# A new order for the front of a graph-convolution and expert kernel, and other PSUM banks for three aggregations

## The chip, the cores and the metric

The kernel runs on one core of a Trainium2 chip. A core has a matrix engine (TensorE, PE in the profile; its weight loads are PEld), a vector engine (VectorE, DVE), a scalar engine (ScalarE, ACT), a general one (GpSimd, POOL) and a sequencer that issues transfers (SyncE, SP). Each runs its own instructions in order; they meet through semaphores. Matrix results land in PSUM, in eight banks of 128 rows by 2 KB; all else lives in SBUF. The metric is the device time of one execution in microseconds (us), and lower is better.

## The reference

625 rows x of 1024 numbers pass through two blocks with a residual each. The first is a relational graph convolution over 20,000 edges (source, destination, one of two types), the second a mixture of experts (8 experts, the best 2 of each row, and 2 shared ones). Cut to what matters here:

```python
x = x + gnn(layernorm(x));  x = x + ffn(layernorm(x))

def gnn(h):                                   # h: 625 x 1024
    n = ln_weight * (h * rsqrt(mean(h**2) + 1e-6))
    out = n @ W_root + bias                   # 1024 x 286
    for r in range(2):
        w = (edge_type == r)
        msg = n[src] @ W_rel[r] * w[:, None]
        sums = segment_sum(msg, dst);  cnt = segment_sum(w, dst)
        out = out + sums / maximum(cnt, 1)[:, None]
    return h + elu(out) @ wo
```

## The kernel before

Rows are worked in five tiles of 125. The kernel never gathers messages. It counts edges instead: a matrix CT holds, for each relation, how many edges lead from each source row to each destination row, and the sum over edges becomes a product of CT with the projected rows P = n @ W_rel[r]. CT comes from one-hot matrices. The edge list is cut into 160 chunks of 125 edges; for each chunk DVE makes a one-hot of the source's place in its tile (`ohs`, an equality at L849 and a product at L850) and one of the destination's key (`ohk`, L852), and PE multiplies them into an accumulator `cnt` (L868, two banks). Chunks go in groups of 4 (the first sixteen) and 8, with eight buffers for the one-hots.

The work before 100 us, the front, has these pieces:

- Loads. SP issues edge types and sources, then x's tile 0, W_root, x's tile 1, tiles 2 and 3, tile 4 in two parts, the two W_rel, wo (L545 to L654). ACT issues destinations and ln_weight. POOL issues small ones, among them conv_bias broadcast to 125 rows (L610).
- `edge_columns` (L664): DVE makes rows of keys and sources, PE transposes them into one bank (`p_edge`), ACT and DVE write the three columns `cols` that the one-hots compare with.
- `warm(n)` (L970): n products of a constant with itself into `scrap`, whose result nobody reads. They stand at the start of PE's queue.
- `stats(t)` (L753): DVE takes mean and variance of tile t and `neg`, the negative mean; ACT writes h = x - mean (L765).
- `to_columns(t)` (L789): PE transposes h in eight blocks into two banks, ACT evicts the first four with the ln weight as scale (L801), DVE the other four (L798). The result is `nT`. The row factor 1/std is put in later, because it can be taken out of a product: `scales(a, b)` works it out for a few tiles at once.
- `project(i)` (L886): eight steps of nT with a weight matrix, first W_root for tiles 0 to 4 (i = 0 to 4), then relation 0, then relation 1. Root results become `agg` on DVE with the bias `cb` (L901), the others P in three bf16 parts.
- `aggregate(d, r)` (L904): 15 products of CT and P, divided by the count and added to `agg` (L915). Then `elu`, `elu_columns` and `output_proj`.

Which piece goes where is written by hand. `count_windows` runs over the chunks, and after chunk c it runs what `at(c, ...)` has put there: stats and to_columns of tile t, project i, and so on (L987 to L1021). The build then orders the instructions of each engine by its own estimate, within the dependencies and within `tc.issue_after`, which holds an instruction behind another; so an instruction's place may differ from the program's by some steps. `stats(0)` stands behind the edge columns, the first one-hots behind `stats(0)`, `stats(1)` behind tile 0's eviction.

PSUM has a ring of three banks `acc` (scrap, projections, later the output), one of three `mm` (transposes, aggregations) and two for `cnt`. Before `aggregate(4, 1)` the pool is closed and a new one opened with five `acc` and three `mm` (L1031 to L1033), over the same eight banks.

## Time and profile before

| | us |
|---|---|
| median of 3 runs | 304.25 (303.66 to 304.46) |
| the profiled execution, whole | 303.7 |
| its span, first to last instruction | 301.4 |
| PE busy | 290.8 |
| DVE busy | 168.4 |
| ACT busy | 107.5 |
| first transposes of x (tile 0) start | 10.62 |
| project(0) starts | 11.79 |
| aggregate(4, 1) starts | 100.16 |

An execution is some 2.3 us longer than its span. Busy time counts an engine's instructions, weight loads apart; matrix products overlap, so that a busy PE may still hide short waits between its products. In lists by time the columns are start, duration, engine, line, operation, output and inputs, shape, number, and in brackets the idle time before and what ended it. Line numbers are those of the kernel before.

### The profile page before, as it was taken

The numbers are of one execution on the slowest core, as the hardware profiler recorded it, in microseconds if no ns is written. First come the engines' busy times: TensorE is split into PE (matmuls) and PEld (weight loads), VectorE is DVE, ScalarE is ACT, GpSimd is POOL, SyncE is SP. The second block draws the span as 40 slices with busy tenths as digits, with TensorE's granted clock in tenths as the row PEclk, the third lists the DMA queues.
The fourth block names the chain that finished last, engine by engine and source line by source line (L and its number), as shares of the span: only waits on it lengthen the run. The fifth ranks groups of instructions, "written<-read, shape, count | busy, mean of one in ns | idle before, by whom it ended". The sixth has DMA issues, their size and how long they took to land.

```text
span 301.4 us, 4682 instructions
## 1 busy us (share of the span) xinstructions
PE 290.8 (96%) x1649; PEld 194.9 (65%) x1649; DVE 168.4 (56%) x465; ACT 107.5 (36%) x246; POOL 45.2 (15%) x98
## 2 busy tenths in 40 slices
PE   8799999999999799999999999999999999999993
PEld 6687777787889534376777887887843334444452
DVE  5999999998327668756883122212223211255921
ACT  2455118355334432155123244638359311000000
POOL 9500000000000014240131212210003222200000
PEclk9999999999999999999999999999999999999998
DMA  7999910000009999965999253340057555479442
GB/s 243 304 318 393 421 65 2 0 2 1 0 17 340 348 348 391 400 195 182 348 396 410 86 203 96 114 141 3 0 190 276 221 209 210 191 291 385 161 138 73
DMA packets 27408, 61.15 MB, mean 203 GB/s; under 512 B 2176, under 2 KB 16007, under 8 KB 27375
## 3 DMA queue, kind: packets, MB, share of 16 engines
q1 hardware_dynamic: 21806, 43.77, 40.7%
q0 software_dynamic: 5280, 16.69, 15.7%
q10 hardware_dynamic: 294, 0.35, 0.5%
q8 instruction: 15, 0.25, 0.3%
q14 instruction: 13, 0.10, 0.1%
HBM read 42.76 MB, written 18.81 MB: 204 GB/s over the span
## 4 chain that ended last, share of the span: by engine, by line
PE 93%; DVE 4%; ACT 1%; issue 0%; ACTq 0%
PE p_pr L891 20%; PE p_h L1359 13%; PE p_yj L1417 13%; PE p_o L1472 11%; PE p_sh L1137 10%; PE p_y L952 6%; PE p_agg L909 6%; PE p_x L1340 3%; PE p_t L795 3%; PE cnt L868 2%; PE p_y L956 2%; PE p_hT L1371 1%; PE scrap L972 1%; PE p_gate L1085 1%; PE p_o L1474 1%; DVE ln_4s L727 0%
## 5 line engine op out<-in xcount | busy, mean ns | idle before, releaser
L891 PE MATMUL p_pr<-wg,nT 128*125 128x286 f32 x240 | 62.5, 409 | 0.0
L891 PEld LDWEIGHTS p_pr<-wg,nT 128*125 128x125 f32 x240 | 43.2, 187 | 11.3 <-ACT nT L801 0.2
L1359 PE MATMUL p_h<-w1a,xsT 128*128 (+2 forms) x176 | 40.0, 380 | 0.0
L1417 PE MATMUL p_yj<-w2a,hjT 128*128 (+2 forms) x88 | 38.6, 594 | 0.0
L1472 PE MATMUL p_o<-sw,shT 128*125 128x512 f32 (+1 forms) x88 | 36.1, 553 | 0.0
L1137 PE MATMUL p_sh<-h2T,sw 128*128 128x313 f32 (+1 forms) x128 | 35.2, 428 | 0.0
L1359 PEld LDWEIGHTS p_h<-w1a,xsT 128*128 128x128 f32 (+2 forms) x176 | 28.7, 168 | 7.4 <-issue 0.5
L1137 PEld LDWEIGHTS p_sh<-h2T,sw 128*128 128x128 f32 x128 | 23.6, 189 | 8.6 <-issue 0.2
L1417 PEld LDWEIGHTS p_yj<-w2a,hjT 128*128 128x128 f32 (+2 forms) x88 | 14.4, 168 | 22.4 <-issue 22.4
L1472 PEld LDWEIGHTS p_o<-sw,shT 128*125 128x125 f32 x88 | 16.4, 187 | 16.9 <-issue 16.2
L1421 DVE COPY ys<-p_yj 128x512 f32<-128x512 f32 x15 | 10.4, 692 | 28.7 <-PE p_yj L1417 26.5
L1363 DVE COPY hj<-p_h 128x256 f32<-128x256 f32 x11 | 4.7, 425 | 30.8 <-PE p_h L1359 30.8
L909 PE MATMUL p_agg<-P,CT 125*125 125x287 bf16 x150 | 20.1, 287 | 1.6 <-DVE agg L915 1.6
L966 POOL DMA_DIRECT2D x1d<-xh x10 | 5.3, 532 | 98.5 <-DVE xh L959 98.5
L909 PEld LDWEIGHTS <-CT 125*125 125x125 bf16 x150 | 18.5, 136 | 2.5 <-issue 2.0
L1425 POOL DMA_INDIRECT yt<-ys,row x11 | 10.8, 984 | 50.5 <-DVE ys L1421 50.5
L952 PE MATMUL p_y<-wo_t,eT 128*125 128x512 f32 x40 | 18.1, 595 | 0.0
L1332 POOL DMA_INDIRECT xs<-h2d,tok x11 | 11.2, 1015 | 45.0 <-PE p_x L1340 30.9
L1374 ACT ACTIVATE hjT<-p_hT,vT 128x128 f32<-128x128 f32 (+2 forms) x34 | 8.7, 332 | 24.5 <-PE p_hT L1371 24.5
L1344 DVE COPY xsT<-p_x 128x512 f32<-128x512 f32 x11 | 7.6, 692 | 17.4 <-PE p_x L1340 13.8
L1448 DVE SCALAR_TENSOR_TENSOR x<-p_o,x 125x512 f32<-125x512 f32 (+1 forms) x11 | 6.9, 641 | 16.3 <-PE p_o L1474 16.3
L1359 PE MATMUL p_h<-w1m,xsT 128*64 128x256 f32 (+1 forms) x96 | 14.7, 381 | 0.0
(302 smaller groups left out, 424.0 us busy)
## 6 DMA issues: line engine op xcount, KB each, us to landing
w1a<-in_L_ffn_W_dram SPq DMA_DIRECT2D x8, 1024.0 KB, 10.5
w2a<-in_L_ffn_W_dram SPq DMA_DIRECT2D x8, 1024.0 KB, 4.8
yt<-zero SPq DMA_DIRECT2D x2, 2560.0 KB
g<-yt SPq DMA_DIRECT2D x10, 512.0 KB, 6.7
sw<-in_L_ffn_sW_dram SPq DMA_DIRECT2D x4, 1024.0 KB, 5.0
x<-x1d SPq DMA_DIRECT2D x5, 500.0 KB
wg<-in_L_gnn_W_rel_dram SPq DMA_DIRECT2D x2, 1144.0 KB, 19.1
x1d<-xh POOLq DMA_DIRECT2D x5, 448.0 KB, 6.7
```

The source lines that it names most:

```text
L795: nc.tensor.transpose(pv[:, k, :], row[:, at : at + 128], ident[:TP, :TP])
L891: nc.tensor.matmul(p[:TP, :F], nT[:, k, m * TP : (m + 1) * TP], wg[:, k, r, :], start=(k == 0), stop=(k == KD - 1))
L909: nc.tensor.matmul(p[:TP, : F + 1], CT[:, m, at : at + TP], P[:, m, r, i], start=(m == 0 and i == 0), stop=(m == NT - 1 and i == 2))
L952: nc.tensor.matmul(ps[s][:TP, :], eT[:, k, :], wo_t[:, k, s * 512 : (s + 1) * 512], start=(k == 0), stop=False)
L1137: nc.tensor.matmul(p[:, : z - a], sw1[:, i, k, t * 128 : (t + 1) * 128], h2T[:, k, a:z], start=(k == 0), stop=(k == KD - 1))
L1332: nc.gpsimd.indirect_dma_start(out=xs, out_offset=None, in_=h2d, in_offset=bass.IndirectOffsetOnAxis(ap=tok[:, j : j + 1], axis=0))
L1340: nc.tensor.transpose(p[:, k * 128 : (k + 1) * 128], xs[:, at : at + 128], ident)
L1359: nc.tensor.matmul(p[a:b, :H], xsT[j][:, k, a:b], w1m[j, a][:, 0, k, :] if a else w1a[:, bass.ds(e, 1), k, :], start=(k == 0), stop=(k == ...
L1417: made = nc.tensor.matmul(p[a:b], hjT[:, j, k, a:b], w2m[j, a, k][:, at] if a else w2a[:, bass.ds(e, 1), k, at], start=(k == 0), stop=(k = ...
L1421: nc.vector.tensor_copy(y[:, at], p)
L1425: sent.append(nc.gpsimd.indirect_dma_start(out=yt, out_offset=bass.IndirectOffsetOnAxis(ap=row[:, j : j + 1], axis=0), in_=y, in_offset=No ...
L1472: nc.tensor.matmul(p[:TP, :n], shT[:, i, k, own], sw2[:, i, k, at], start=(i == 0 and k == 0), stop=False)
```

## The change

Six edits, made together:

- Loads: x's tile 1 is loaded ahead of W_root, and W_root comes in two halves.
- The bias is loaded once as a single row (`cb1`, by ACT's queue) and spread over 125 rows by a product with a row of ones, evicted by ACT; the broadcast load on POOL is gone.
- Edge lists: sources and keys are transposed into two banks. The columns of the sources are now worked out in a function of their own, `source_columns`, which is issued behind `stats(0)`, and all on DVE.
- The first two tiles: `stats(0)` is held behind the last cast of the edge rows alone. For tiles 0 and 1 h is written in two pieces, 384 columns by ACT and 640 by DVE.
- Order: `to_columns(0)` follows 22 warming products instead of 40 and a first group of one-hots; the one-hots of group 0, `stats(1)`, `scales(0, 2)` and `project(0)` stand ahead of the first count product. Later pieces move to other chunks.
- Banks: `aggregate(1, 1)`, `(3, 1)` and `(4, 1)` take a bank of the ring `acc` instead of `mm`.

```diff
+    cb1 = fbig.tile([1, F], F32, name="cb1")
+    nc.scalar.dma_start(cb1, conv_bias.rearrange("(o f) -> o f", o=1))
...
-    def load_w(r, w):
-        nc.sync.dma_start(wg[:, :, r, :], w.rearrange("(k p) f -> p k f", p=128))
+    def load_w(r, w, *ks):
+        for k in ks or (slice(0, KD),):
+            nc.sync.dma_start(wg[:, k, r, :], w.rearrange("(k p) f -> p k f", p=128)[:, k])

     load_x(0, 1)
-    load_w(R, W_root)
     load_x(1, 1)
+    load_w(R, W_root, slice(0, KD // 2), slice(KD // 2, KD))
...
     cb = gbig.tile([TP, F], F32, name="cb")
-    nc.gpsimd.dma_start(cb, bcast_rows(conv_bias, TP))
+    one = fbig.tile([1, TP], F32, name="one")
+    nc.vector.memset(one, 1.0)
...
-        p = ps_mm("p_edge")
+        got = nc.vector.tensor_copy(rowf[:, 0], rows_i["src"])
+        ps = [ps_acc("p_edge"), ps_mm("p_edge_k")]
...
+    def source_columns(v, behind):
+        q = fbig.tile([EP, 2, EC], F32, name="q")
+        with tc.issue_after(behind.ins):
+            nc.vector.tensor_scalar(q[:, 0], v, -float(TP // 2), 1.0 / TP, op0=ALU.add, op1=ALU.mult)
         nc.vector.tensor_scalar(q[:, 1], q[:, 0], ROUND, -ROUND, op0=ALU.add, op1=ALU.add)
-        nc.scalar.copy(column(cols[:, SP_]), pairs(q[:, 2]))
+        nc.vector.scalar_tensor_tensor(cols[:, SP_], pairs(q[:, 1]), -float(TP), pairs(v),
+                                       op0=ALU.mult, op1=ALU.add)
...
+        p = ps_mm("p_cb")
+        nc.tensor.matmul(p[:TP, :F], one, cb1, start=True, stop=True)
+        nc.scalar.copy(cb, p[:TP, :F])
...
-            with tc.issue_after((second[0] if t > 1 else evicted[1] if t else behind).ins):
+            with tc.issue_after((second[0] if t > 1 else first if t else behind).ins):
...
+        own, rest = (slice(0, 384), slice(384, D)) if t < 2 else (slice(0, D), None)
...
-            moved = nc.scalar.activation(h, xh[:TP, t, :], AF.Identity, bias=neg)
+            moved = nc.scalar.activation(h[:, own], xh[:TP, t, own], AF.Identity, bias=neg)
+        if rest:
+            with tc.issue_after(last.ins):
+                last = nc.vector.tensor_scalar(h[:, rest], xh[:TP, t, rest], neg, None, op0=ALU.add)
...
-        p = ps_mm(f"p_agg_{d}_{r}")
+        p = (ps_acc if r and d in (1, 3, 4) else ps_mm)(f"p_agg_{d}_{r}")
...
-    warm(40)
-    ahead = stats(0)
+    warm(22)
+    source_columns(sources, stats(0))
+    to_columns(0, hs[0], nT, True)
...
-    for t, (c0, c1) in enumerate(((0, 3), (4, 9), (13, 19), (16, 22), (20, 26))):
+    for t, (c0, c1) in enumerate(((0, 3), (6, 11), (9, 14), (13, 18))):
         if t:
-            at(c0, stats, t)
-        at(c1, to_columns, t, None, nT, True)
+            at(c0, stats, t + 1)
+        at(c1, to_columns, t + 1, None, nT, True)
...
-    at(6, scales, 0, 2)
-    at(18, scales, 2, 4)
-    at(21, scales, 4, NT)
-    for i, c in enumerate((7, 15, 21, 24, 28, 46, 64, 82, 100, 118, 134, 148)):
-        at(c, project, i)
+    at(10, scales, 2, 4)
+    at(14, scales, 4, NT)
+    for i, c in enumerate((3, 12, 15, 20, 38, 56, 74, 92, 110, 128, 146)):
+        at(c, project, i + 1)
...
+    oh_s, oh_k, first = one_hots(0, GROUPS[0])
+    made[0] = oh_s, oh_k
+    stats(1)
+    scales(0, 2)
+    project(0)
     count_windows(between)
```

The one-hots' code is moved into a function `one_hots`, in which the destination's one-hot is held behind the source's product, and the first two groups behind tile 0's eviction and tile 1's statistics.

More of the change, by code (lines that the diff above doesn't have):

```diff
@@ L671, in edge_columns, with pairs @@
                                        op0=ALU.mult, op1=ALU.add)
-        nc.vector.tensor_copy(rowf[:, 0], rows_i["src"])
-        p = ps_mm("p_edge")
-        pv = p[:EP, : 2 * EC].rearrange("p (a j c) -> p a j c", a=2, j=2)
+        got = nc.vector.tensor_copy(rowf[:, 0], rows_i["src"])
+        ps = [ps_acc("p_edge"), ps_mm("p_edge_k")]
         for a in (0, 1):
             for j in range(2):
-                nc.tensor.transpose(pv[:, a, j, :], rowf[:, a, j * EP : (j + 1) * EP], ident[:EH, :EH])
-        wide = [EP, EH, 2, 2]
-        def column(v):
-            return v.rearrange("p (c j) b -> p c j b", j=2)
-        def pairs(v):
-            return v.rearrange("p j c -> p c j")[:, :, :, None].to_broadcast(wide)
-        with tc.issue_after(table.ins):
-            nc.scalar.copy(column(cols[:, KW_]), pairs(pv[:, 1]))
-        q = fbig.tile([EP, 3, 2, EH], F32, name="q")
-        nc.vector.tensor_scalar(q[:, 0], pv[:, 0], -float(TP // 2), 1.0 / TP, op0=ALU.add, op1=ALU.mult)
+                nc.tensor.transpose(ps[a][:EP, j:EC:2], rowf[:, a, j * EP : (j + 1) * EP], ident[:EH, :EH])
+        with tc.issue_after(table.ins):
+            nc.scalar.copy(cols[:, KW_], pairs(ps[1][:EP, :EC]))
+        return got, ps[0][:EP, :EC]
+    def pairs(v):
+        return v[:, :, None].to_broadcast([EP, EC, 2])
+    def source_columns(v, behind):
+        q = fbig.tile([EP, 2, EC], F32, name="q")
+        with tc.issue_after(behind.ins):
+            nc.vector.tensor_scalar(q[:, 0], v, -float(TP // 2), 1.0 / TP, op0=ALU.add, op1=ALU.mult)
         nc.vector.tensor_scalar(q[:, 1], q[:, 0], ROUND, -ROUND, op0=ALU.add, op1=ALU.add)
-        nc.vector.scalar_tensor_tensor(q[:, 2], q[:, 1], -float(TP), pv[:, 0], op0=ALU.mult, op1=ALU.add)
-        nc.scalar.copy(column(cols[:, SP_]), pairs(q[:, 2]))
-        return nc.vector.tensor_scalar(column(cols[:, VV_].bitcast(I16)), pairs(q[:, 1]), 4096.0, 7168.0,
+        nc.vector.scalar_tensor_tensor(cols[:, SP_], pairs(q[:, 1]), -float(TP), pairs(v),
                                        op0=ALU.mult, op1=ALU.add)
+        nc.vector.tensor_scalar(cols[:, VV_].bitcast(I16), pairs(q[:, 1]), 4096.0, 7168.0,
+                                op0=ALU.mult, op1=ALU.add)
     flagf = const.tile([1, 2], F32, name="flagf")
@@ L826, in sparse_kernel, with one_hots, both, halves @@
     ends = [R * TP * min(DB * (b + 1), NT) for b in range((NT + DB - 1) // DB)]
+    made = {}
+    def one_hots(c0, g):
+        oh_s = oneh.tile([EP, MAXG, 128], F16, tag="oh_s", name=f"ohs_{c0}")
+        oh_k = oneh.tile([EP, MAXG, KR], F16, tag="oh_k", name=f"ohk_{c0}")
+        def both(what, n):
+            return [EP, g, n // 2, 2], cols[:, what, c0 : c0 + g][:, :, None, :].to_broadcast([EP, g, n // 2, 2])
+        def halves(v):
+            return v.rearrange("p g (a b) -> p g a b", b=2)
+        row = iota[:EP].rearrange("p (a b) -> p a b", b=2)
+        shape, key = both(SP_, 128)
+        os = halves(oh_s[:, :g, :])
+        with ExitStack() as order:
+            if c0 < 8:
+                order.enter_context(tc.issue_after((second[0] if c0 else evicted[1]).ins))
+            nc.vector.tensor_tensor(os, row[:, None].to_broadcast(shape), key, op=ALU.is_equal)
+        last = nc.vector.tensor_tensor(os, os, both(VV_, 128)[1], op=ALU.mult)
+        shape, key = both(KW_, KR)
+        with tc.issue_after(last.ins):
+            nc.vector.tensor_tensor(halves(oh_k[:, :g, :]), row[:, None, :SPAN].to_broadcast(shape), key,
+                                    op=ALU.is_equal)
+        return oh_s, oh_k, last
     def count_windows(between):
@@ L831, in count_windows @@
         for g in GROUPS:
-            oh_s = oneh.tile([EP, MAXG, 128], F16, tag="oh_s", name=f"ohs_{c0}")
-            oh_k = oneh.tile([EP, MAXG, KR], F16, tag="oh_k", name=f"ohk_{c0}")
-            def both(what, n):
-                return [EP, g, n // 2, 2], cols[:, what, c0 : c0 + g][:, :, None, :].to_broadcast([EP, g, n // 2, 2])
-            def halves(v):
-                return v.rearrange("p g (a b) -> p g a b", b=2)
-            order = ExitStack()
-            if c0 == 0:
-                order.enter_context(tc.issue_after(ahead.ins))
-            elif c0 == 8:
-                order.enter_context(tc.issue_after(second[0].ins))
-            row = iota[:EP].rearrange("p (a b) -> p a b", b=2)
-            shape, key = both(SP_, 128)
-            os = halves(oh_s[:, :g, :])
-            nc.vector.tensor_tensor(os, row[:, None].to_broadcast(shape), key, op=ALU.is_equal)
-            nc.vector.tensor_tensor(os, os, both(VV_, 128)[1], op=ALU.mult)
-            shape, key = both(KW_, KR)
-            nc.vector.tensor_tensor(halves(oh_k[:, :g, :]), row[:, None, :SPAN].to_broadcast(shape), key,
-                                    op=ALU.is_equal)
-            order.close()
+            oh_s, oh_k = made.pop(c0) if c0 in made else one_hots(c0, g)[:2]
             for i in range(g):
@@ L975, in sparse_kernel @@
     warm(24)
-    behind = edge_columns()
+    behind, sources = edge_columns()
     transpose_lnw()
-    warm(40)
-    ahead = stats(0)
+    warm(22)
+    source_columns(sources, stats(0))
+    to_columns(0, hs[0], nT, True)
     after = {c: [] for c in range(EC)}
```

## Prediction, made blind

> **What bounds the kernel now.** I read four views in turn: busy time by engine, who waited for whom on TensorE (PE), the first 32 us in order of time, and the chain of work that ended last. Busy time first:

> ```profile
> PE 290.8 (96%) x1649; PEld 194.9 (65%) x1649; DVE 168.4 (56%) x465; ACT 107.5 (36%) x246; POOL 45.2 (15%) x98
> ```

> PE is the bound, so a change pays only where PE idles or does useless work. Its waits up to 106 us (us in total, times, longest):

> ```profile
> PE cnt L868 <- DVE ohs L850: 1.7, 1, 1.7
> PE p_agg L909 <- DVE agg L915: 1.6, 1, 1.6
> PE cnt L866 <- DVE nil L824: 1.5, 1, 1.5
> ```

> The 1.5 us are the launch. The change aims at the other two: the front's start, and one aggregation. The front in order of time (start, duration):

> ```profile
> 3.93 0.29 DVE L672 CAST rowf<-src_i 80x250 f32<-80x250 int32 x1
> ...
> 7.68 1.28 DVE L757 BATCH_NORM_STATS2 st<-xh 125x6 f32<-125x512 f32 x2
> ...
> 9.42 1.15 ACT L765 ACTIVATE h<-xh,neg 125x1024 f32<-125x1024 f32 x1 [1.40 <-DVE neg L760]
> ...
> 10.62 1.07 PE L795 MATMUL p_t<-ident,h 125*128 125x125 f32 x8
> ...
> 18.46 0.14 DVE L760 TENSOR_SCALAR neg<-mv 125x1 f32<-125x1 f32 x1
> ...
> 24.99 1.15 ACT L765 ACTIVATE h<-xh,neg 125x1024 f32<-125x1024 f32 x1 [1.01 <-DVE neg L760]
> ...
> 31.30 1.05 PE L795 MATMUL p_t<-ident,h 125*128 125x125 f32 x8
> ```

> VectorE (DVE) waits from 4.22 to 6.57 for the edge lists' transposes and their copy, and reaches tile 0's statistics only at 7.68. PE's warming matmuls end at 8.61, it idles 1.69 us, and project(0) starts at 11.79. From there PE never waits. But stage by stage (columns: length, then busy time of PE, PEld, DVE, ACT, POOL, clock, DMA share, GB/s):

> ```profile
> 7.00:9.00 2.00, 1.61 (x29) 1.44 (x26) 1.93 (x6) 0.46 (x1) 1.16 (x3) 1.00 1.10 170
> 12.00:60.00 48.00, 47.96 (x315) 37.01 (x315) 47.76 (x131) 20.39 (x54) 2.25 (x9) 1.00 0.59 210
> 60.00:84.00 24.00, 24.00 (x168) 19.95 (x168) 16.67 (x38) 11.64 (x34) 0.00 (x0) 1.00 0.00 1
> ```

> From 12 to 60 us DVE is as full as PE, 47.76 of 48 us. It is the second bound: PE can start earlier only as far as DVE keeps feeding it. The first row also shows the transfers drop to 170 GB/s with the DMA engines full. By queue in those 2 us:

> ```profile
> q0 software_dynamic: 33, 0.14, 80.7%
> q1 hardware_dynamic: 174, 0.20, 29.8%
> ```

> 0.14 MB on q0, the conv bias read 125 times (139.6 KB), took 80.7% of 16 engines for 2 us, some 1.6 us of all transfers. Last, the chain at the second wait:

> ```profile
> 96.11 0.17 ACT deg L911
> ...
> 98.74 0.46 DVE el L928
> ...
> 99.50 0.53 DVE agg L915
> 100.03 0.14 issue
> 100.16 2.05 PE p_agg L909 x15
> ```

> **The change part by part.** Durations are this execution's: 303.7 us in all, span 301.4; the median of the runs is 304.25, so I carry the difference over to the median.

> *Transfers.* SP issues one DMA more (W_root in halves, 0.4 us of issue as its neighbours at 0.42-0.43) and x's tile 1 ahead of W_root; POOL issues one less (0.81 us); ACT one more, 1x286 (0.58 us as L531), behind which stand only the table load and a scalar that nobody awaits. The trace's landing records have x's tile 0 at 5.7, W_root at 10.7, tile 1 at 11.9, tiles 2-3 at 15.0. Without the 1.6 us on q0, and at the 370-380 GB/s of the windows from 4 to 7 us, I estimate tile 1 (0.52 MB) at 7.1, the halves (0.59 MB each) at 8.7 and 10.3, tiles 2-3 (1.05 MB) at 12.9. project(0) needs the halves at 9.5 and 11.6, tile 2's statistics theirs at 13.7, so 0.8 us and more of cover each. POOL no longer waits 2.34 us for the bias; its two b2/sb2 copies (0.12 MB) move up by some 3 us into these loads, at most 0.3 us at 380 GB/s. Ends: if the gap on q0 stays, 1.6 us later; if x's tile 0 had long been there, no earlier than its last byte, about 4.8.

> *Tile 0.* DVE goes from the cast (4.22) straight to tile 0's statistics, at 5.8 when it lands: 0.60+0.68 (two statistics), aggregate 0.21, neg 0.15 with handovers of 0.04, so neg at 7.5 (9.39 before). The subtraction is split: ACT does 384 of 1024 columns, 1.15x384/1024 + 0.1 = 0.5; DVE 640, from L731's tensor_scalar (0.81 for 1024) 0.51-0.56. Both end near 8.1; transposes start at 8.2 for 10.62. ACT now copies the keys' columns (0.43), lT (0.17) and the bias (0.50, as L895's 286 from PSUM) behind its part of h: 8.1 to 9.0. That covers the 0.75 us that passed before between first transpose and first eviction, so it is free, by 0.05 us. First nT piece 0.36, project(0) at 9.5-9.7. **2.1 us earlier.** Eight count matmuls that ran ahead of it before (0.03 each) now come after: 2.1-0.2 = 1.9 net. The bias product (8 columns of lnw took 0.27; one 128x286 f32 step 0.5) stands in place of 18 warming matmuls (0.056 each, 1.0): PE waits there anyway, cost nothing; without that cover 0.5.

> *Tile 1.* DVE after 8.1: the source columns, 0.33+0.25+0.5+0.32 (the third is new as 320 wide from PSUM; L692 took 0.32 for 160, L915 0.52 for 286) to 9.5; nT's half 0.67 to 10.2; three one-hots 0.42+0.42+0.27 to 11.2; statistics to 12.8; its half of h 0.55 to 13.4. PE ends project(0) (4.1) at 13.6-13.7. It just fits. Transposes and first piece 1.1 us later: project(1) at 14.7 for 16.9.

> *Tiles 2 to 4, where most is lost.* DVE's own balance: it starts 0.8 us earlier (5.8 for 6.57) and loses its 0.58 us wait at 11.2, but takes 2x0.55 of h, 0.5 of source columns in place of ACT's 0.46 and 0.32 of its own, and some 0.3 of new handovers in a row: 1.4 gained, 1.6 added. **DVE's throughput point does not move.** Walking its new order, start to start: from 13.4 to tile 2's neg stand four one-hots of 0.33 and one of 0.19, two statistics of 0.6, an nT of 0.6, seven small ones of 0.07 and an aggregate of 0.12, 3.9 us: 17.3 (18.46 before). In the same way neg of tile 3 at 19.8 (22.30), of tile 4 at 24.6 (24.80). ACT's h of tile 2 still meets PE at 18.8. Tile 2's first eviction stands behind a square root on ACT: PE waits 0.35. In the new order three of tile 3's transposes stand behind two steps of project(2): h at 21.3, PE waits 0.3. Three of tile 4's stand ahead of project(3); before they came at 31.3, 5 us after h (24.99+1.15 = 26.14). h of tile 4 is again at 26.1, and PE waits 0.6. With 0.2 each ahead of or inside projects 0, 1 and 4 that is 1.85 us of waits. Before had such waits inside its projects too: 4.10, 3.98, 4.09, 4.12, 4.09 in the chain against 3.94 undisturbed, 0.7 us. Lost: 1.85-0.7 = 1.15. Left: 0.75-0.95 at the first relation product. Up to 60 us PE then asks for count groups ahead of a full DVE; with projects placed eight chunks earlier among the counts I take another 0 to 0.3, middle 0.1.

> *Banks.* aggregate(1,1), (3,1), (4,1) go to the ring of three that the projections leave free. The page names one p_agg wait, the 1.55 us before (4,1). In the built program of the change (4,1) still waits for the eviction of (3,1), because it is the first tile of a new PSUM pool, which waits for the old pool's last users whatever ring. (1,1) and (3,1) never waited. **Worth 0**; ends: 0.1 slower, or 1.6 faster if that wait went (then the column transpose of tile 2, el at 99.45, is next).

> Sum: -1.9 + 1.15 + 0.1 + 0 = -0.65; with handovers at 0.07 instead of 0.04, which fits the front of before better, the same walk gives -0.95. I take **-0.8: 302.9 on the profiled execution, 303.45 on the median**.

> [...] Rows: 24 warming matmuls took 2.74 us, the next 40 took 2.41, so PE doubles its rate after some 3 us; the 1.69 us of idle and eight transposes before project(0) did not undo it. The changed front has fewer warming matmuls and about 2.1 us between the last one and project(0), less than the 3.2 of before, so by the rows nothing. [...]

> **Rivals.**
> 1. *The whole start gets through*: the built waits matter less than I think and PE gains 1.9-2.1, or tile 0 landed early (0.5 more). For: PE waited for nothing from 11.79 on. Against: DVE full, tile 3's h at 23.7 met its transposes at 23.77 already. 304.25-1.9 = 302.3.
> 2. *A wash*: DVE binds to 60 us and returns all: 304.2. For: 1.4 gained against 1.6 added. Against: in before tile 4 and the one-hots had slack.
> 3. *Slower: tiles 2-3 of x land late.* DVE is in order and comes to tile 2's statistics at 13.7; behind them stand tile 1's eviction and all one-hots, so each us of lateness beyond about 13.8 is a us of PE. At the 227 GB/s seen from 14 to 15 us they would land at 14.6-15; from 14.7 on the change loses. At 15.6: +0.9, 305.1. For: the rate did drop there, for no reason that I can name. Against: estimate 12.9.

> **How the numbers follow.** Forecast (gain 0.4-1.4) 0.6; whole start 0.13; wash 0.13; late x 0.14 (0.12 of it past 0.9). 0.3% (0.9 us) is about what a measurement tells from no change. Half of the forecast's chance lies above 0.9: faster 0.3+0.12 = 0.42; slower 0.12; same 0.46. Range: from rival 1 to 0.45 above the median, 302.3 to 304.7; beyond lies 1 in 10 on either side.

> **What would show it.** First transposes near 8.2-8.5 and project(0) near 9.5-9.8; no packets of 80.7% on q0; PE waits of 0.3-0.6 on ACT's h and nT between 18 and 27 us; DVE still full to 60; the p_agg wait of 1.5 us still there. Wrong would be: no waits at tiles 3 and 4 (more gain), a DMA named before tile 2's statistics, or warming at half rate behind 9.5.

## The result: no change, where 0.8 us were forecast

| | before | changed |
|---|---|---|
| median of 22 runs each, us | 304.27 (303.48 to 305.72) | 304.57 (302.92 to 305.67) |
| ratio to before | | 1.000, interval 0.9986 to 1.0013 |
| the profiled execution; its span | 303.7; 301.4 | 304.58; 302.4 |
| project(0) starts | 11.79 | 11.34 |
| aggregate(4, 1) starts | 100.16 | 101.30 |

The stated range held the time, but the forecast itself, 0.8 us faster, did not come. The profiled execution shows why in its first 28 us. TensorE (PE), in order of time (start, duration), first one row of the kernel before, then the changed kernel:

```profile
6.21 2.41 PE L972 MATMUL scrap<-iota 128*128 128x128 f16 x40
```

```profile
5.12 0.65 PE L680 MATMUL p_edge<-ident,rowf 80*125 80x80 f32 x2
...
6.25 1.29 PE L744 MATMUL p_cb<-cb,one 1*125 1x286 f32 x2
7.47 2.53 PE L988 MATMUL scrap<-iota 128*128 128x128 f16 x22
9.79 1.46 PE L806 MATMUL p_t<-ident,h 125*128 125x125 f32 x8
11.34 3.88 PE L906 MATMUL p_pr<-wg,nT 128*125 128x286 f32 x15
```

Before, 40 warming products behind the edge lists took 2.41 us. Now 22 of them take 2.53: 0.107 us from start to start for 0.056, half the rate. By the trace's record of the granted clock PE went to full rate only at 10.68 here, at 6.22 before. (That record begins with the first rise, so the clock column in the tables by stage reads 1.00 ahead of it whatever the rate was; there the spacing of the products has to tell.) The bias product ahead of them took 1.29 us for the 0.5 that I had put down. VectorE (DVE) in the same execution:

```profile
5.72 1.29 DVE L763 BATCH_NORM_STATS2 st<-xh 125x6 f32<-125x512 f32 x2 [1.46 <-DMA xh<-in_x_dram]
...
7.48 0.65 DVE L776 TENSOR_SCALAR h<-xh,neg 125x640 f32<-125x640 f32 x1
...
11.36 0.68 DVE L809 TENSOR_TENSOR nT<-p_t,lT 128x500 f32<-128x500 f32 x1 [1.93 <-ACT nT L812]
```

h of tile 0 is there at 8.13, as predicted (8.1). PE takes it up only at 9.79, because the warming products stand ahead of it. So DVE, which had to be the early one, waits 1.93 us for the transposes. The chain of the work that ended last goes the same way:

```profile
6.39 1.15 PE p_cb L744 x2
7.54 2.46 PE scrap L988 x22
10.00 1.26 PE p_t L806 x8
11.36 0.68 DVE nT L809
...
26.59 0.14 issue
26.73 1.15 ACT h L773
27.92 0.54 PE p_t L806 x3
```

Between 11.36 and 26.53 every piece of that chain is DVE's (left out here). What PE lost at its start DVE lost too, and DVE carries it down to tile 4. Stage by stage (length, busy time of PE, PEld, DVE, ACT, POOL, clock, DMA share, GB/s):

```profile
7.00:9.00 2.00, 2.00 (x17) 1.53 (x16) 1.83 (x7) 1.30 (x4) 1.52 (x4) 1.00 1.08 371
12.00:60.00 48.00, 47.40 (x311) 36.03 (x310) 47.37 (x133) 18.81 (x51) 0.50 (x6) 1.00 0.57 200
```

The transfers did gain: 371 GB/s in the first row for 170 before. DVE is as full to 60 us as it was. PE's waits up to 106 us (in total, times, longest):

```profile
PE cnt L881 <- DVE nil L835: 1.6, 1, 1.6
PE p_agg L925 <- DVE agg L931: 1.6, 1, 1.6
PE p_t L806 <- ACT h L773: 0.4, 1, 0.4
```

The second is the wait before aggregate(4, 1): the new banks changed nothing.

### The profile page after: what moved, and what is told of

It reads as the page before. It is cut to its first block, busy times and chain, and to the rows that moved or that the text cites. A ratio compares the mean times of both kernels' runs of the same rounds, so it can differ in the third digit from the quotient of the medians.

```text
span 302.4 us, 4653 instructions
## 1 busy us (share of the span) xinstructions
PE 292.9 (97%) x1633; PEld 195.2 (65%) x1633; DVE 169.7 (56%) x468; ACT 106.9 (35%) x246; POOL 44.4 (15%) x97
## 4 chain that ended last, share of the span: by engine, by line
PE 89%; DVE 8%; ACT 1%; issue 1%; DVEq 0%; ACTq 0%
PE p_pr L906 16%; PE p_h L1380 13%; PE p_yj L1438 13%; PE p_o L1493 11%; PE p_sh L1158 10%; PE p_y L968 6%; PE p_agg L925 6%; PE p_x L1361 3%; PE p_t L806 2%; PE p_y L972 2%; PE scrap L988 2%; DVE st L763 2%; PE cnt L883 2%; PE p_hT L1392 1%; PE p_gate L1106 1%; PE p_o L1495 1%
## 5 line engine op out<-in xcount | busy, mean ns | idle before, releaser
L906 PE MATMUL p_pr<-wg,nT 128*125 128x286 f32 x240 | 63.6, 411 | 0.2
L1158 PEld LDWEIGHTS p_sh<-h2T,sw 128*128 128x128 f32 x128 | 23.7, 189 | 8.6 <-issue 0.2
L1493 PEld LDWEIGHTS p_o<-sw,shT 128*125 128x125 f32 x88 | 16.4, 187 | 16.9 <-issue 16.2
L1442 DVE COPY ys<-p_yj 128x512 f32<-128x512 f32 x15 | 10.4, 692 | 28.7 <-PE p_yj L1438 26.5
L982 POOL DMA_DIRECT2D x1d<-xh x10 | 5.4, 542 | 101.3 <-DVE xh L975 101.3
L1365 DVE COPY xsT<-p_x 128x512 f32<-128x512 f32 x11 | 7.6, 692 | 17.0 <-PE p_x L1361 14.7
L1380 PE MATMUL p_h<-w1m,xsT 128*64 128x256 f32 (+1 forms) x96 | 14.7, 381 | 0.0
```

The costliest lines, as they stand in the source:

```text
L906: nc.tensor.matmul(p[:TP, :F], nT[:, k, m * TP : (m + 1) * TP], wg[:, k, r, :], start=(k == 0), stop=(k == KD - 1))
L1158: nc.tensor.matmul(p[:, : z - a], sw1[:, i, k, t * 128 : (t + 1) * 128], h2T[:, k, a:z], start=(k == 0), stop=(k == KD - 1))
L1380: nc.tensor.matmul(p[a:b, :H], xsT[j][:, k, a:b], w1m[j, a][:, 0, k, :] if a else w1a[:, bass.ds(e, 1), k, :], start=(k == 0), stop=(k == ...
L1442: nc.vector.tensor_copy(y[:, at], p)
L1493: nc.tensor.matmul(p[:TP, :n], shT[:, i, k, own], sw2[:, i, k, at], start=(i == 0 and k == 0), stop=False)
```

## The experiments

My theory after the result, W, was that PE's clock had eaten the gain: the rate doubles only at the end of a window of a fixed grid, and the new start fills the window badly. In the two traces the clock's record has the full rate for 293.546 us before and 290.133 changed, 3.413 apart, and 86 and 85 times that. Its main rival, V, was my rival 2: DVE is full to 60 us and returns whatever PE gains. A third, P, was that the bias product costs by its own length.

One thing makes the profiles comparable. From the start of aggregate(4, 1) to the start of PE's last product the nine traces with two PSUM pools all take 195.79 us, the same to 0.01; the five with one pool, as below, take 0.2 more. So the start of aggregate(4, 1) tells what the front did in an execution. From the last product's start to the end it was 5.3 to 6.4 us in them, in no relation to an edit. Ratios are to the kernel before, run beside on the same chip; the starts (us) are those of the profiled execution. The first row is the kernel before against itself: a ratio of 1.002, or 0.6 us, arises there without any change.

| kernel | ratio, interval | project(0) | aggregate(4, 1) |
|---|---|---|---|
| kernel before, again | 1.002, 0.9994 to 1.0045 | 11.91 | 101.20 |
| changed, again | 1.0011, 0.9990 to 1.0031 | 10.15 | 100.56 |
| warming early | 0.9997, 0.9970 to 1.0025 | 9.81 | 101.44 |
| 8 warming products | 1.0008, 0.9988 to 1.0027 | 10.29 | 101.70 |
| bias on POOL's queue | 1.0025, 1.0006 to 1.0045 | 11.11 | 101.75 |
| tile 4 held | 1.0005, 0.9982 to 1.0028 | 11.35 | 101.54 |
| changed, one PSUM pool | 0.9958, 0.9930 to 0.9987 | 11.14 | 99.37 |
| before, one PSUM pool | 0.9968, 0.9935 to 1.0000 | 12.46 | 100.04 |
| start alone | 0.9997, 0.9979 to 1.0015 | 9.41 | 100.63 |
| first combination | 0.9910, 0.9877 to 0.9943 | 9.76 | 100.56 |
| second combination | 0.9945, 0.9922 to 0.9969 | 9.54 | 98.95 |
| third combination | 0.9891, 0.9856 to 0.9926 | 9.55 | 97.75 |

**The kernel before, unchanged.**

> The kernel before, unchanged, timed against itself, to see how it stands to the moment at which PE's clock doubles. Theory W (the clock's window): PE doubles its rate only where a window of some 3.4 us, whose grid runs freely against the kernel's start, ends after enough work on PE. In the changed kernel's profile the 22 warming products took 2.53 us (0.107 each, half rate), in the kernel before 40 took 2.41 (0.056). W expects this kernel to be nearly blind to the grid, since its forty products in a row fill a window in any phase and stand in a gap of 1.69 us: 304.3, and no more than 0.5 us between runs of different phase. Theory V (VectorE is full to 60 us and returns whatever PE gains) and theory P (the bias product, 1.29 us, is what costs) say 304.3 too and have no reason for phases.

Median 305.26 beside 304.92. The expectation of at most 0.5 us between runs fell: they spread over 2.9 us. In this profile PE's 40 warming products took 3.13 us, but with 0.96 us still idle behind them, as W has it. What was late was x: DVE waited 0.9 us for it and PE 0.5 for nT, and aggregate(4, 1) came at 101.20 for 100.16. Late loads moved this kernel by some 0.9 us here, so single profiles must be compared at the place of an edit.

**Warming ahead of the edge lists.**

```diff
-    warm(24)
+    warm(34)
     behind, sources = edge_columns()
     transpose_lnw()
-    warm(22)
```

> The changed kernel with 34 warming products ahead of the edge lists' transposes and none behind the bias product (24 and 22 before). W: the products now run without a break from 2.6 us to 6.2 at half rate, so a window with 2 to 2.5 us of work in it ends in most phases before 8, and even a cold start ends the bias product at 8.75 in place of the warming at 10.0: 1.0 to 1.5 us faster than the changed kernel's 304.57 in the median, 303.1 to 303.5, with few runs above 304.5. V: PE starts earlier, VectorE returns it by 60 us, 304.3 to 304.6. P: the bias product still stands ahead of the first transposes, no gain, 304.5.

0.9997, no gain. PE in order of time, and then the stages with their clock (third column from the right):

```profile
7.04 0.72 PE L744 MATMUL p_cb<-cb,one 1*125 1x286 f32 x2
8.65 1.07 PE L806 MATMUL p_t<-ident,h 125*128 125x125 f32 x8 [0.89 <-ACT cols L683]
9.81 5.81 PE L906 MATMUL p_pr<-wg,nT 128*125 128x286 f32 x16
```
```profile
6.70:10.00 3.30, 2.32 (x15) 1.55 (x15) 2.79 (x9) 1.90 (x7) 2.67 (x7) 1.00 1.11 370
10.10:13.40 3.30, 3.30 (x8) 2.30 (x8) 3.16 (x9) 0.67 (x3) 2.22 (x8) 0.50 1.11 393
13.50:17.00 3.50, 3.47 (x23) 2.63 (x22) 2.03 (x7) 1.22 (x6) 0.00 (x0) 1.00 0.99 226
```

This is the clock's window seen by itself. The rate went up at 6.64, the bias product took 0.72 us, and after 3.413 us with 0.25 us of products besides it and the transposes PE was set back to 0.50, from 10.06 to 13.47: project(0) took 5.81 us for 4.1. And DVE waited 1.23 us for x's tile 2.

**Fewer warming products.**

```diff
-    warm(22)
+    warm(8)
```

> The changed kernel with 8 warming products behind the bias product in place of 22. A rival to W, theory Q (queue): the rate does not matter, the 22 products are only too long; without 14 of them the first transposes come at 8.4 in place of 9.8, so 1.4 us faster than the changed kernel in every run, 303.2. W: the start comes earlier, but in the phases that are cold at 7.5 us the next window holds too little work and project(0) runs its first 2 to 4 us at half rate, which costs 1 to 2 us of the 1.4: median 304.2 to 305.0, with the spread between runs as wide as the changed kernel's 2.7 us or wider. V: 304.3.

1.0008, no gain. The first transposes of x came at 8.57, but took 1.93 us for 1.07, and project(0) took 5.58 for 4.1:

```profile
8.57 1.93 PE L806 MATMUL p_t<-ident,h 125*128 125x125 f32 x8
10.29 5.58 PE L906 MATMUL p_pr<-wg,nT 128*125 128x286 f32 x16
```

The queue theory falls: the rate matters, and PE was not at full rate before 13.4.

**The bias as before.**

```diff
-    cb1 = fbig.tile([1, F], F32, name="cb1")
-    nc.scalar.dma_start(cb1, conv_bias.rearrange("(o f) -> o f", o=1))
...
+    nc.gpsimd.dma_start(cb, bcast_rows(conv_bias, TP))
...
-        nc.tensor.matmul(p[:TP, :F], one, cb1, start=True, stop=True)
```

> The changed kernel with the bias loaded as before, broadcast on POOL's queue, and no product for it. W (the clock's window, as the profiles of the first experiments show it: a window of 3.4 us sets the full rate if some 2.2 us of it held products other than transposes): without the 1.2 us of the bias product ahead of them, the warming products from 6.2 us on and those up to 5.1 leave only 1.1 us uncovered, so every window that ends between 5.9 and 8.6 holds 2.2 us and PE is at full rate by 8.9 in nearly every run; the first transposes come at 8.2 to 8.7 in place of 9.8. Against it stand 1.6 us of transfers on q0, which by the step Transfers bring W_root's halves to 10.3 and 11.9, up to 0.8 us behind project(0)'s need. Together 0.3 to 1.3 us faster than the changed kernel, ratio to before 0.9965 to 0.9990, and few runs above the level of before. V (VectorE returns the gain): 1.000. P (the bias product is what costs, by its own length alone): 0.5 to 1.2 us faster in every phase, 0.9965.

1.0025, no gain; as the kernel before against itself gave 1.002, slower is not shown. The first transposes came at 8.36, and PE was at full rate from 6.6. Then PE stood still, as did DVE later (both in order of time, with what ended the idle time in brackets):

```profile
11.11 4.09 PE L900 MATMUL p_pr<-wg,nT 128*125 128x286 f32 x16 [1.68 <-DMA wg<-in_L_gnn_W_root_dram]
```
```profile
16.05 0.69 DVE L757 BATCH_NORM_STATS2 st<-xh 125x6 f32<-125x512 f32 x1 [1.89 <-DMA xh<-in_x_dram]
```

The gain of 0.5 to 1.2 us that theory P expected did not come, but this run does not settle P, for the broadcast that came back has a cost of its own. The step Transfers had its price right: with the broadcast on q0 PE waits 1.68 us for W_root, where 1.6 were put down for it.

**Tile 4's transposes held** behind project(3)'s last product, `third[0]`.

```diff
+            with ExitStack() as order:
+                if scaled and t == NT - 1:
+                    order.enter_context(tc.issue_after(third[0].ins))
```

> The changed kernel with the transposes of tile 4 held behind the last product of project(3) (three of them stood ahead of it and waited 0.39 us for h, and by the counts of products PE loses 0.7 us between the starts of project(2) and project(3)). The step Tiles 2 to 4 says that this order loses 0.6: 0.4 to 0.7 us faster than the changed kernel, ratio to before 0.9980 to 0.9990. If VectorE is what PE waits for anyway (V), the wait moves to project(4) or to the counts: no change, 1.000.

1.0005: no change, as V forecast, but not by V's cause. The 0.39 us for h are gone from the list of PE's waits, and in their place stands a wait ahead of project(3) for ACT's copy of tile 3's transposes:

```profile
PE p_pr L909 <- ACT nT L815: 0.6, 1, 0.6
```

**One PSUM pool.**

```diff
-        return psum[0].tile([128, 512], F32, tag="acc", name=name, bufs=nacc[0])
+        taken[0] += nacc[0] == 5
+        late = nacc[0] == 5 and taken[0] % 5 in (4, 0)
+        return psum[0].tile([128, 512], F32, tag="cnt" if late else "acc", name=name, bufs=2 if late else 3)
...
-    banks_of.close()
-    psum[0] = ctx.enter_context(tc.tile_pool(name="psum2", bufs=1, space=bass.MemoryType.PSUM))
+    ctx.enter_context(banks_of)
```

> The changed kernel without the second PSUM pool: the ring acc goes on as five banks, the three that it had and the two of the counts, inside the one pool. The question is the step Banks: whether the 1.55 us before aggregate(4, 1) are the pool's wait for its last users, as I said, or the bank's. If the pool's: the wait goes, aggregate(4, 1) starts at 99.8 in place of 101.3, nothing later waits for it, 1.4 to 1.6 us faster than the changed kernel's 304.57, 303.1. If it only moves to the next tile (the transpose of el for tile 2, or the output projection): 0 to 0.5 faster, 304.1 to 304.6.

The same edit on the kernel before, where aggregate(4, 1) stays in the ring `mm`:

> The kernel before, with the ring acc extended by the two banks of the counts inside the one PSUM pool, and aggregate(4, 1) in the ring mm as before. If the pool's end is all that the 1.55 us wait for, they go here too: 1.4 to 1.6 us faster than before, ratio 0.9948 to 0.9955, and the Banks edit is not needed for it. If the bank is a second cause (aggregate(4, 1) would get the bank of a tile that is still read), the wait stays, 1.000, or a part of it, 0.997.

0.9958 and 0.9968. PE of the changed kernel with one pool, in order of time:

```profile
97.16 2.03 PE L929 MATMUL p_agg<-P,CT 125*125 125x287 bf16 x15
99.02 0.51 PE L960 MATMUL p_elT<-ident,el 125*128 125x125 f32 x3
99.37 2.03 PE L929 MATMUL p_agg<-P,CT 125*125 125x287 bf16 x15
...
101.92 0.20 PE L711 MATMUL p_deg<-deg,onec 125*1 125x10 f32 x2 [0.20 <-ACT deg L931]
```

The kernel before with one pool:

```profile
97.82 2.03 PE L913 MATMUL p_agg<-P,CT 125*125 125x287 bf16 x15
99.69 0.51 PE L944 MATMUL p_elT<-ident,el 125*128 125x125 f32 x3
100.04 2.03 PE L913 MATMUL p_agg<-P,CT 125*125 125x287 bf16 x15
```

aggregate(4, 1) starts 2.21 and 2.22 us behind its forerunner, where it was 3.93 in both kernels with two pools. 1.7 us go, 0.2 come back at `p_deg`. So it was the change of pools that cost the wait, in either ring. Whether the new pool's first tile waits for all users of the old one, or only for a bank that it happens to share with one of them, these runs don't tell apart.

**The first combination**: one pool, tile 4 held, 24 warming products behind the edge lists, and the bias by SP's queue:

```diff
     load_x(2, 2)
+    cb = gbig.tile([TP, F], F32, name="cb")
+    nc.sync.dma_start(cb, bcast_rows(conv_bias, TP))
```

> The changed kernel with all three at once: one PSUM pool with a ring of five, tile 4's transposes held behind project(3), and the bias broadcast by SP's queue behind x's tiles 2 and 3, with 24 warming products from 6.2 us on and no product for the bias. W: full rate by 8.9 in nearly every run, so the start gains 1.0 to 1.5 over the changed kernel, the pool 1.5, tile 4 0.4 to 0.7: 301.2 to 301.9 where before has 304.3, ratio to before 0.990 to 0.992. V: the start's gain goes by 60 us, only the pool's is left: 0.995.

0.991 as W had it, median 301.96, but its profile is of a run at 305.03. There project(1) still starts at 14.91, and then DVE waits for x (in total, times, longest; the longest is before tile 2's statistics, at 16.52):

```profile
DVE st L761 <- DMA xh<-in_x_dram: 4.4, 2, 2.5
```

**The start alone**, with the copies of b2 and sb2 sent to SP's queue, behind wo:

```diff
-    nc.gpsimd.dma_start(bd[:, :NS, :], bass.AP(tensor=sb2.tensor, offset=sb2.offset,
...
+    nc.sync.dma_start(bd[:, :NS, :], bass.AP(tensor=sb2.tensor, offset=sb2.offset,
...
```

> The changed kernel with two edits at its start: the bias is broadcast by SP's queue behind x's tiles 2 and 3 (no product for it; 24 warming products follow the edge lists), and the two copies of b2 and sb2, whose packets of 32 KB took 1.4 us each between 12 and 15 us beside x's tiles 2 and 3, go from POOL's queue to SP's, behind wo. W: PE at full rate by 8.9 in nearly every run, and VectorE waits for x's tile 2 in few: first transposes at 8.2 to 8.7, 1.0 to 1.5 us faster than the changed kernel, ratio to before 0.995 to 0.9965, with few runs above 304. V: VectorE returns it by 60 us, 0.999 to 1.001. If the late tiles of x are not due to those copies: half the runs at 304 to 305 as for the bias on POOL's queue, 0.999.

**The second combination** is the same with one pool and tile 4 held:

> The same start with the one PSUM pool and its ring of five, and tile 4's transposes held behind project(3) (which alone changed nothing). W: 301.2 to 301.9 where before has 304.3, ratio 0.990 to 0.992, and without the run at 305 that the version with the copies on POOL's queue had: the spread between runs within 1.5 us. If the late tiles of x have another cause, the spread stays at 3 to 4 us and the ratio at 0.991.

**The changed kernel again** ran beside them:

> The changed kernel once more, beside the two others on one chip, for its spread over the phases of the clock's window. W: runs with a window that ends between 5.5 and 6.5 us after the start 302.9 to 303.4 if before has 304.3 (three in ten), the others 304.2 to 305.7; ratio to before 0.998 to 1.001. V: no such two groups.

0.9997, 0.9945 and 1.0011. W as the only cause falls here. All three profiles had the full rate early (from 5.2, 8.1 and 5.9 us), project(0) came at 9.41, 9.54 and 10.15, and the start alone was still no faster. The second combination gained about the pool's 1.5 us and no more. Nor did the changed kernel's runs fall into two groups (303.85 to 305.89, the profiled one, with its full rate from 5.9, at 304.97). The start alone has a new collision. DVE and then POOL in it, in order of time:

```profile
8.40 1.67 DVE L691 TENSOR_SCALAR q<-q 125x160 f32<-125x160 f32 x1
```
```profile
8.63 0.26 POOL L622 TENSOR_TENSOR join<-join,ident 128x32 f32<-128x32 f32 x1
8.82 0.24 POOL L889 MEMSET P<- 125x30 bf16 x1
8.88 1.04 POOL L1006 MEMSET zero<- 128x1024 f32 x1
9.88 0.26 POOL L622 TENSOR_TENSOR join<-join,ident 128x32 f32<-128x32 f32 x1
```

With the copies gone from POOL's queue its zero fill moved from 11.27 to 8.88, onto a DVE step of 0.27 us, which now took 1.67 and ended about when the fill did. Tile 1's neg came at 13.88 for the 12.8 of the walk. The second combination has the same step at 1.68 us. The profile of the changed kernel again shows nothing of this, but two small lags, one in DVE's list by time and one in PE's waits:

```profile
14.86 0.69 DVE L763 BATCH_NORM_STATS2 st<-xh 125x6 f32<-125x512 f32 x1 [0.48 <-DMA xh<-in_x_dram]
```
```profile
PE p_t L806 <- ACT cols L683: 0.8, 1, 0.8
```

The second is the bias product's other cost, which I had not seen. By the program it takes the third bank of the ring `mm`, so that tile 0's transposes need the bank of the keys, which ACT empties only behind h. So the product has a cost there after all, if not the one that P meant.

**The third combination**: one pool, 24 warming products, the bias by SP's queue, tile 4 not held, and

```diff
-    load_x(2, 2)
+    load_x(2, 1)
+    cb = gbig.tile([TP, F], F32, name="cb")
+    nc.sync.dma_start(cb, bcast_rows(conv_bias, TP))
+    load_x(3, 1)
...
     def clear():
+        with tc.issue_after(second[0].ins):
+            nc.vector.memset(zero[:1, :1], 0.0)
         nc.gpsimd.memset(zero, 0.0)
```

(the one-element fill on DVE holds POOL's fill until 34.67), with the copies of b2, sb2 and rW on SP's queue.

> The changed kernel with the one PSUM pool, 24 warming products and the bias broadcast by SP's queue (as in the two versions before), and three edits against what took back the early start in their profiles: x's tiles 2 and 3 are loaded one by one (VectorE waited up to 2.53 us for both), the copies of b2, sb2 and rW go to SP's queue behind wo, and the zero fill of POOL (1.04 us) is held until some 40 us, because a VectorE step of 0.27 us took 1.67 and ended with that fill. Theory S (the start is given back by such meetings on VectorE's path, not by VectorE's own work): tile 1's h by 13.6, project(1) at 14.6 to 15.0, project(3) at 26.5 to 27.0 where before has 27.3 with one product more of the counts, so 0.7 to 1.1 us kept of the start and 1.5 of the pool: ratio to before 0.9915 to 0.993, 301.9 where before has 304.3. Theory V (VectorE's own work returns it in any case): project(3) not before 27.4, only the pool's 1.5 us, 0.995.

0.9891, median 301.25 beside 304.33, faster than both kernels, and a little more than theory S forecast. Theory V's 0.995 falls. Of the 3.1 us between the medians the profiles show 2.2: 0.69 at aggregate(2, 0) and 1.5 from the pool; the rest lies in runs without a profile. PE and then DVE in order of time:

```profile
8.39 1.07 PE L805 MATMUL p_t<-ident,h 125*128 125x125 f32 x8 [0.67 <-ACT h L772]
9.55 4.12 PE L905 MATMUL p_pr<-wg,nT 128*125 128x286 f32 x16
...
14.76 4.12 PE L905 MATMUL p_pr<-wg,nT 128*125 128x286 f32 x16
```
```profile
17.32 0.14 DVE L765 TENSOR_SCALAR neg<-mv 125x1 f32<-125x1 f32 x1
...
19.77 0.14 DVE L765 TENSOR_SCALAR neg<-mv 125x1 f32<-125x1 f32 x1
...
24.61 0.15 DVE L765 TENSOR_SCALAR neg<-mv 125x1 f32<-125x1 f32 x1
```

The prediction had 8.2, 9.5-9.7 and 14.7, and 17.3, 19.8 and 24.6 for these starts. aggregate(2, 0), a place at which all kernels have done the same products but for the warming and the bias, starts at 76.33 (77.02 before). So theory S holds for the three edits together; which of them was needed how far was not tried one by one. The profile shows no DVE wait for x after tile 0, and no long step.

## What the prediction had right and wrong, step by step

The gain of 0.8 us did not come because two steps of the sum failed, *Tile 0* and *Transfers*. That 304.57 still lay inside the stated range was luck: the sum had put both losses at nothing, and together they happened to take back about what the rest gained. The predicted 76.2 for aggregate(2, 0) is 77.02 less the forecast 0.8.

| start, us | predicted | before | changed | changed, again | third combination |
|---|---|---|---|---|---|
| project(0) | 9.5-9.7 | 11.79 | 11.34 | 10.15 | 9.55 |
| project(1) | 14.7 | 16.89 | 16.49 | 15.31 | 14.76 |
| neg of tile 2 | 17.3 | 18.46 | 19.00 | 18.39 | 17.32 |
| neg of tile 4 | 24.6 | 24.80 | 26.35 | 25.64 | 24.61 |
| aggregate(2, 0) | 76.2 | 77.02 | 78.16 | 77.43 | 76.33 |

- *Tile 0* failed, in the sentence that the bias product "stands in place of 18 warming matmuls (0.056 each, 1.0): PE waits there anyway, cost nothing". The forty products were not idle filling: in all three profiles with them PE was at full rate by 7.8 us (6.22, 7.77 and 6.45), with the 22 at 5.9 to 11.2. In the profiled execution the product (0.8 more than its 0.5) and 22 products at half rate put project(0) 1.8 us later than the 9.55 of the third combination. From there the delay passes on whole: the third combination's -0.69 at aggregate(2, 0) plus 1.8 is 1.11, where the changed kernel shows +1.14. I had read from the rows that PE doubles its rate after some 3 us of products; in the changed kernel it had not done so after 46. By the clock's record rises and falls lie whole multiples of 3.413 us apart, in before, in the changed kernel and in the one with the early warming (last section). A rate lost again shows, of all the fronts, only in the one with the early warming, from 10.06 to 13.47. In the changed kernel full rate was not reached until 10.68.
- *Transfers* failed for tiles 2-3: I estimated 12.9 and "0.8 us and more of cover". By the landing records they were there at 14.38 in the changed kernel's profile, before DVE, itself late, came to them at 15.48. Where DVE waited for them it got them at 14.86 (changed, again), 15.26 (warming early), 16.05 (bias on POOL's queue) and 16.52 (first combination). That is rival 3's mechanism, and with the rate at full it is what took much of the rest: in the changed kernel again 0.6 us at project(0) (x's tile 0 at 6.26, 0.3 later than in the third combination, and the bank of the keys) and 0.48 at tile 2 make 1.08, of the 1.10 by which its aggregate(2, 0) is behind the third combination. The packets of 32 KB that the copies of b2 and sb2 set beside them, which I had put at 0.3 us at most, took 1.2 to 1.4 us each; how much of the lateness they make, and why the rate falls at 13 to 15 us, stays open.
- *Tile 1* and *Tiles 2 to 4* were right where neither of the two intervened: in the third combination the walk along DVE held to 0.1 us. Of the 2.24 us by which project(0) was early there (some 0.24 of them the eight count products that now come later), 0.69 were left at aggregate(2, 0): 1.3 lost, where I had 1.15 and 0.1 for the counts. The single waits are seen only in part: for h of tile 4 I put down 0.6, and PE's lists have 0.4 in the changed kernel and 0.34 in the third combination.
- *Banks* was right: the edit was worth nothing, and the change of pools was the reason, as the runs with one pool show.
- Rival 2, the wash, is what the median shows, but not by its mechanism: of its own DVE's path returned some 1.3 us, as the sum had it, and not all; beyond that it passed on what the clock and the loads had held up. This is read from two profiles of the changed kernel. How the causes share out over its other runs, which form no two groups, stays open.

## What to carry to other kernels

Useless products at the start are a budget of time on a clock whose phase differs from run to run: in the two profiles of the changed kernel the rise came at 10.68 and at 5.86 us. Ask which window they fill, and count what replaces them by the same measure; and when the start of a kernel moves forward, look again at every load and fill that had been hidden beside the old start, on every queue. A wait that names an engine at a place where a pool is closed and reopened can be the pool's: keeping one pool, with a ring over five banks, took 1.7 us away here, 1.5 net.
